# A graph network on one core: the second half of the gates' layer norm stands in the next graph's gates

## The chip, the cores and the metric

The kernel runs on one core of a Trainium2 chip. The metric is device time in microseconds (us) of one execution. The core has five engines that run at the same time, each through its own queue, in the order of that queue: PE (TensorE, matrix products), DVE (VectorE), ACT (ScalarE), POOL (GpSimd) and SP (SyncE, which here only issues transfers). An instruction that waits holds up all that stands behind it in its queue. Transfers (DMA) are issued from the queues of SP, ACT and POOL.

## The reference

The input is 64 graphs of 256 nodes with 256 features, and one 256 x 256 adjacency matrix for each. Two layers follow one another, each with a residual and a layer norm without weights:

```python
def _layernorm(x, axis=-1, eps=1e-5):
    m = jnp.mean(x, axis=axis, keepdims=True)
    v = jnp.var(x, axis=axis, keepdims=True)
    return (x - m) / jnp.sqrt(v + eps)
...
x = _layernorm(x + _L0_gnn_ref(x, adj, ...), axis=-1)
x = _layernorm(x + _L1_gnn_ref(x, adj, ...), axis=-1)
```

Layer 0 is a product with the normalised adjacency matrix and one with a weight matrix. Layer 1 has a convolution branch (a 1 x 1 convolution, then one of 17 taps along the nodes, a residual), a message branch (attention from distances, times messages), and a GRU cell that joins them:

```python
x_in = jnp.concatenate([x_conv, x_nmp], axis=-1)
gi = x_in @ w_ih.T + b_ih
gh = x @ w_hh.T + b_hh
...
r = jax.nn.sigmoid(gi_r + gh_r)
z = jax.nn.sigmoid(gi_z + gh_z)
nn_ = jnp.tanh(gi_n + r * gh_n)
return (1.0 - z) * nn_ + z * x
```

The last line, plus the residual, goes through the second layer norm and is the output. "The gates" below are the GRU cell with that norm.

## The kernel before, in words

The graphs are worked on in four groups (`q`) of 16 (`Q`). A group passes through: layer 0 and the branches of layer 1 for each graph (`layer0`, `layer1`); the products of the long convolution in a transformed domain, for all 16 graphs at once (`products`); the inverse transform, which is DVE work (`complex_end` and what it calls); and the gates graph by graph (`gates`, `gru`). The groups overlap. Each of these is a Python generator that gives control back at every `yield`; a part between two yields is called a piece here. The driver at the end of the kernel interleaves the pieces of one group's gates with the pieces of the next group's `layer0` and `layer1`, with steps of `products`, and (through `paced`) with steps of the inverse transform, which are issued behind instructions that were marked with `mark`. The gates of the last group run after all else, beside the rest of the inverse transform and then alone.

The framework sets the semaphores. It also orders each engine's queue by itself: an instruction that comes earlier in the program takes precedence, but one that is ready may pass one that isn't. `tc.issue_after` forces an instruction behind another one on its engine; `behind`, called in `transposed` for some graphs, does so for all later DVE instructions with respect to a transposition (L812).

`gru(g)` has four pieces. The matrix products (L856) follow a scheme with seven products of 128 x 384 blocks in place of eight, so that some of their operands are sums of blocks that POOL makes beforehand (`input_sums`, L838), and that DVE adds results (L873, L874, L882, L884, L921).

- Piece 1: the load of the next graph's inputs (L787, and L790 for one channel); products p1 and p7; ACT copies p1 (L867).
- Piece 2: product p6, two additions on DVE (L873, L874), the rest of p1, which ACT copies (L876).
- Piece 3: `transposed(g + 1)` (on PE with L824 on ACT, or on DVE at L812 with L813 on POOL and L816 on ACT), the load of this graph's residual into a tile `x1_g` of which there are two (`load_x1`, L794 on SP's queue), product p5 and the rest of p7, additions L882 and L884, three of the next graph's sums on POOL.
- Piece 4: the rest of p5, the fourth sum, a load for the graph after the next one (`load_conv`, L777 or L783), the squashing of the r and z gates on ACT (L897, twice), and `finished`: six elementwise steps on DVE (L905 to L915) with a tanh on ACT (L913), then the layer norm in place on the `x1_g` tile, and the store of the result, issued from ACT's queue (L917).

The layer norm (`layernorm`, L325 to L333) is a generator with one yield. Before it: mean and variance by DVE for two chunks of 128 nodes (L325, L326), an addition (L327), and the power -0.5 on POOL (L328), which gives `ln_rs`. Behind it: the product of the mean with that factor on DVE (L331, `ln_mr`) and the application on ACT, one instruction for each chunk (L333). Its small tiles have four buffers each. In layer 0 the driver takes the two halves at different pieces: statistics at piece 6 of one graph's `layer1`, the rest at piece 2 of the next one. In the gates both halves run in one go (`run`, L916).

For the very last graph the two chunks are finished one after the other.

Of the kernel before, what the change touches and what calls it, by code (L numbers as in the profile page):

```python
# [14 lines left out]
P = 128  # L15
LN_EPS = 1e-5
# [10 lines left out]
def kernel(  # L27
# [27 lines left out]
    nc = tc.nc  # L55
# [35 lines left out]
    def mark(op, gates=0):  # L91
        marks.append((op.ins, gates))
# [7 lines left out]
    def behind(op):  # L100
        order.close()
        order.enter_context(tc.issue_after(op.ins))
# [664 lines left out]
    def in_blocks(g):  # L767
        return g % Q < EARLY or g >= B - Q
# [23 lines left out]
    def load_x1(g):  # L792
        OWN[g] = gate.tile([P, NCH, D], F32, name="x1_g")
        nc.sync.dma_start(OWN[g], x1_d[g // Q][g % Q].rearrange("(c p) d -> p c d", p=P))  # L794
# [12 lines left out]
    def transposed(g):  # L807

        inputs = GATE[g]
        xcT = inputs[:, 2 * DCH :]  # L810
        if in_blocks(g):
            behind(nc.vector.transpose(xcT.rearrange("p k (s r) -> p k s r", r=RB), CONV.pop(g)))  # L812
            nc.gpsimd.tensor_tensor(xcT, xcT, inputs[:, 0 : 2 * DCH : 2 * DCH - 1], op=ALU.add)  # L813
            nc.gpsimd.memset(inputs[0:1, 0], 1.0)
            for k in range(DCH):
                nc.scalar.activation(xcT[:, k], xcT[:, k], AF.Relu, bias=bn2_bias[:, k : k + 1])  # L816
            return
        xc = CONV.pop(g)
        p = bank("p_xcT").rearrange("p (k n) -> p k n", k=DCH)
        for k in range(DCH):  # L820
            for c in range(NCH):
                nc.tensor.transpose(p[:, k, c * P : (c + 1) * P], xc[:, c, k * P : (k + 1) * P], ident)
        for k in range(DCH):
            nc.scalar.activation(xcT[:, k], p[:, k], AF.Relu, bias=bn2_bias[:, k : k + 1])  # L824
# [5 lines left out]
    def input_sums(g, *which):  # L830
        A11, A12, A21, A22 = halves(GATE[g])
        S = SUMS.setdefault(g, {})
        for i in which:
# [3 lines left out]
            }[i]  # L837
            nc.gpsimd.tensor_tensor(S[i], x, y, op=op)  # L838

    def gru(g):  # L840

        following = g % Q + 1 < Q
        inputs, S = GATE.pop(g), SUMS.pop(g)
        G = gate.tile([P, NCH, 2, 4, HD], F32, name="G", bufs=1)
        if following:
            load_gate(g + 1)
        A11, A12, A21, A22 = halves(inputs)

        def product(a, b, p=None):
            first = p is None
            if first:
                p = accbank("p_g")
            for k in range(HALF):
                nc.tensor.matmul(  # L856
                    p[:, : 3 * HD] if k == 0 else p[:, HD:], a[:, k], wall[:, b, k].rearrange("p t d -> p (t d)"),
                    start=first and k == 0, stop=True, skip_group_check=not first or k > 0,
                )
            return p  # L860

        def quarter(c, h):
            return G[:, c, h].rearrange("p t d -> p (t d)")

        p1 = product(A11, B11)
        first = gate.tile([P, 4 * HD], F32, name="first", bufs=1)
        nc.scalar.copy(first, p1)  # L867
        p7 = product(S[3], T3)
        yield
        if following:  # L870
            sent(g + 1)
        p6 = product(S[2], T2)
        mark(nc.vector.tensor_add(quarter(0, 1), first, p6), 1)  # L873
        nc.vector.tensor_add(quarter(1, 1), quarter(0, 1), p7)  # L874
        product(A12, B21, p1)
        nc.scalar.copy(quarter(0, 0), p1)  # L876
        yield
        if following:
            transposed(g + 1)
        load_x1(g)  # L880
        p5 = product(S[1], T1)
        mark(nc.vector.tensor_add(quarter(1, 1), quarter(1, 1), p5), 1)  # L882
        product(A22, T4, p7)
        mark(nc.vector.tensor_add(quarter(1, 0), quarter(0, 1), p7), 1)  # L884
        if following:
            input_sums(g + 1, 3, 1, 2)
        yield
        product(S[4], B22, p5)
        if following:
            input_sums(g + 1, 4)  # L890
        if g % Q + 2 < Q:
            load_conv(g + 2)
        x1 = OWN.pop(g)

        def squashed(c):
            rz = G[:, c, :, GR : GZ + 1, :].rearrange("p h t d -> p h (t d)")
            nc.scalar.activation(rz, rz, AF.Tanh, scale=0.5)  # L897

        squashed(1)

        def finished(part):
            both = G[:, part].rearrange("p c h t d -> p (c h) t d")
            chunks = both.shape[1] // 2
            r, z, n, i = (both[:, :, j, :] for j in (GR, GZ, GN, GI))
            nc.vector.scalar_tensor_tensor(n, r, 1.0, n, op0=ALU.add, op1=ALU.mult)  # L905
            i4 = i.rearrange("p (c h) d -> p c h d", h=2)
            bias = bn_t.rearrange("p (h d) -> p h d", h=2).unsqueeze(1).to_broadcast([P, chunks, 2, HD])
            nc.vector.tensor_tensor(i4, i4, bias, op=ALU.add)
            nc.vector.scalar_tensor_tensor(i, n, 0.5, i, op0=ALU.mult, op1=ALU.add)
            y = x1[:, part]  # L910
            yq = y.rearrange("p c (h d) -> p (c h) d", h=2)
            mark(nc.vector.scalar_tensor_tensor(yq, z, 3.0, yq, op0=ALU.add, op1=ALU.mult), 1)
            nc.scalar.activation(i, i, AF.Tanh)  # L913
            nc.vector.scalar_tensor_tensor(i, z, 1.0, i, op0=ALU.subtract, op1=ALU.mult)
            nc.vector.tensor_sub(yq, yq, i)  # L915
            run(layernorm(y, 4 * LN_EPS))  # L916
            nc.scalar.dma_start(out[g].rearrange("(c p) d -> p c d", p=P)[:, part], y)  # L917

        if g == B - 1:
            finished(slice(1, 2))  # L920
        mark(nc.vector.tensor_add(quarter(0, 1), quarter(0, 1), p5), 1)  # L921
        squashed(0)
        finished(slice(0, 1 if g == B - 1 else NCH))
        yield

# [25 lines left out]
    def run(stage):  # L951
        for _ in stage:
            pass
# [103 lines left out]
    def gates(q, part):  # L1057

        for i in part:
            if i == 0:  # L1060
                load_conv(q * Q)
                load_gate(q * Q)
                yield
                load_conv(q * Q + 1)
                sent(q * Q)
                yield
                transposed(q * Q)
                yield
                input_sums(q * Q, 3, 1, 2, 4)
                yield  # L1070
            yield from gru(q * Q + i)

    def nothing():
        return iter(())
# [15 lines left out]
    for q in range(NQ):  # L1090
        first = (q + 1) * Q
        more = q + 1 < NQ
        end = chain(complex_end(q), copies(V2) if more else iter(()))
        if more:
            if q:
                others = [take(late, 3 if i % 3 == 0 else 2) for i in range(AHEAD)]
            else:
                others = [nothing() for _ in range(AHEAD)]
                ALONE.update(range(first, first + AHEAD))
            TILES[0] = V2  # L1100
            begin = graphs(first, range(AHEAD), others)
        KBANK[0] = bank if q else accbank
        sums(0)
        real = real_transform()
        for step in range(STEPS):
            if step < 4:
                run(products(step))
            else:
                run(merge(products(step), take(real, 1)))
                run(complex_begin(step))  # L1110
            if q:
                run(take(late, (0, 1, 1, 1, 1, 1, 2, 1, 2, 1, 2, 1)[step] if more else step % 2))
            else:
                run(take(begin, 3))
        run(real)
        if not q:
            run(paced(begin, end, RATES[q]))
        elif more:
            run(paced(chain(merge(take(late, 20), take(begin, 6), 3), begin), end, RATES[q]))
        else:  # L1120
            run(paced(late, end, RATES[q]))
            run(end)
        if more:
            run(late)
            run(end)
            if q == 0:
                scope.close()
                gate = ctx.enter_context(tc.tile_pool(name="gate", bufs=2))
            early = gates(q, range(EARLY))
            others = [take(early, 5 if q == 0 else 2) for _ in range(Q)]  # L1130
            run(graphs(first, range(AHEAD, Q), others))
            run(early)
            if q == 0:
                scope, AHEAD, V2 = open_ahead(6)
                ctx.enter_context(scope)
            late = gates(q, range(EARLY, Q))
        else:
            run(gates(q, range(Q)))
    order.close()


# [51 lines left out]
```

## Time and profile before

| what | value |
|---|---|
| median of 3 runs | 2126.97 us (2122.22 to 2134.46) |
| the profiled execution's own time | 2127.71 us |
| its span, first to last instruction | 2125.9 us |
| mean granted PE clock in the span | 0.988 |
| L331 on DVE: instructions, median length | 129, 161 ns |
| L333 on ACT in the gates: instructions, median length | 128, 599 ns |
| L328 on POOL: busy, mean length | 94.9 us, 736 ns |
| L838 on POOL (the sums): busy | 139.9 + 70.2 us |
| stores L917: number, size | 63 of 256 KB, 2 of 128 KB |

Of the instructions in this table, all of L917, half of L333 and 65 of the 129 L331 belong to the gates; the others are layer 0's. A group of instructions is written as line, engine, operation, and output<-inputs by the program's names. In a waits view, "A <- B: 7.7, 4, 3.1" says that A's engine stood idle 7.7 us in total, 4 times, at most 3.1 us, until B released it. In an order of time, a line gives the start, the length, the engine, the line of code, the operation and its tiles, how many were merged into it, and in brackets the idle time of the engine before it with what ended it. A wait for several things is put down to the one that came last.

### The profile page before, as it was taken

Reading aid. Unit: us, or ns where it says so; the run is one execution under the profiler, and the core shown is the slowest. Engines: PE = TensorE matmul, PEld = TensorE weight load, DVE = VectorE, ACT = ScalarE, POOL = GpSimd, SP = SyncE. Lnnn points to the kernel's source line nnn. Section 1 sums busy time; section 2 is a strip of 40 time slices with the busy share of each in tenths; the row PEclk is TensorE's granted clock in tenths of the full one; section 3 lists DMA queues with packets and bytes.
Section 4 is the critical chain, followed back from the end, with each engine's and each line's share of the span. In section 5 each row is a group of like instructions: output and inputs, shape, how many; then the busy total and the mean of one; then the engine's idle time right before and its main releaser. Section 6 shows DMA issues by size and latency. Waiting matters only on the chain. (4 is left out here: it accounts for less than half of the span.)

```text
span 2125.9 us, 26260 instructions
## 1 busy us (share of the span) xinstructions
PE 2006.1 (94%) x8157; PEld 1443.2 (68%) x8157; DVE 1474.1 (69%) x3347; ACT 905.3 (43%) x2114; POOL 666.8 (31%) x672
## 2 busy tenths in 40 slices
PE   6999999888999999999999999999999999899997
PEld 5888788766667756667777666667777765555554
DVE  5555567775558788774556888875445889977776
ACT  4666643456432234555553123446554123233333
POOL 3445310121431243223321234323232123344443
PEclk9999999999999999999999999999999999999999
DMA  4766556433437645344335655334323754443331
GB/s 125 230 210 200 192 183 209 154 132 119 122 96 226 194 123 139 114 120 120 94 99 179 201 155 140 118 104 134 96 93 100 243 146 131 111 118 95 93 94 56
DMA packets 305289, 298.05 MB, mean 140 GB/s; under 512 B 84192, under 2 KB 283956, under 8 KB 305150
## 3 DMA queue, kind: packets, MB, share of 16 engines
q1 hardware_dynamic: 245198, 200.37, 32.1%
q10 hardware_dynamic: 44480, 67.39, 8.9%
q0 software_dynamic: 15472, 28.61, 6.0%
q8 instruction: 66, 1.08, 0.2%
q14 instruction: 73, 0.60, 0.1%
HBM read 193.19 MB, written 103.06 MB: 139 GB/s over the span
## 5 line engine op out<-in xcount | busy, mean ns | idle before, releaser
L856 PE MATMUL p_g<-wall,sums 128*128 128x384 f32 x1536 | 537.7, 489 | 11.6 <-DVE G L882 11.6
L856 PE MATMUL p_g<-wall,inputs 128*128 128x384 f32 x1152 | 409.4, 492 | 14.5 <-DVE G L874 14.1
L856 PEld LDWEIGHTS p_g<-wall,sums 128*128 128x128 f32 x1536 | 284.6, 191 | 200.3 <-issue 19.1
L856 PEld LDWEIGHTS p_g<-wall,inputs 128*128 128x128 f32 x1152 | 218.5, 192 | 167.5 <-DVE G L874 23.4
L838 POOL TENSOR_TENSOR sums<-inputs 128x384 f32<-128x384 f32 x128 | 139.9, 1093 | 343.2 <-PE p_g L856 296.9
L369 POOL TENSOR_TENSOR dis<-deg,neg_half 128x2 f32<-128x2 f32 x64 | 48.3, 754 | 475.7 <-DVE deg L367 468.6
L897 ACT ACTIVATE G<-G 128x512 f32<-128x512 f32 x128 | 80.7, 630 | 250.8 <-DVE G L884 148.6
L328 POOL TENSOR_TENSOR ln_rs<-ln_rs,neg_half 128x2 f32<-128x2 f32 x129 | 94.9, 736 | 275.1 <-DVE ln_rs L327 226.7
L541 PE MATMUL p_k<-u,VM 128*128 128x256 f32 x736 | 175.8, 381 | 4.1 <-DMA u<-ud 4.1
L541 PEld LDWEIGHTS p_k<-u,VM 128*128 128x128 f32 x736 | 139.4, 191 | 31.3 <-DMA u<-ud 3.9
L446 PE MATMUL p_conv<-wc,xn 128*128 128x259 f32 x512 | 130.4, 392 | 22.7 <-DVE xn L430 21.5
L399 PE MATMUL p_hT<-adjT,x 128*128 128x256 f32 x512 | 126.7, 391 | 15.6 <-ACT msg L470 8.2
L333 ACT ACTIVATE x_g<-x_g,ln_mr,ln_rs 128x256 f32<-128x256 f32 x128 | 70.0, 593 | 150.3 <-DVE ln_mr L331 148.3
L446 PEld LDWEIGHTS p_conv<-wc,xn 128*128 128x128 f32 x512 | 94.2, 191 | 53.1 <-DVE xn L430 31.1
L508 DVE TENSOR_TENSOR aT<-aT,adjT 128x512 f32<-128x512 f32 x64 | 44.8, 699 | 123.0 <-ACT aT L507 122.8
L409 PE MATMUL p_out<-w,hT 128*128 128x256 f32 x512 | 123.7, 384 | 3.4 <-ACT hT L404 3.0
L482 PE MATMUL p_dft<-fwd,h 128*128 128x240 f32 x512 | 117.4, 372 | 9.2 <-ACT scols L450 8.8
L515 PE MATMUL p_nmp<-aT,msg 128*128 128x256 f32 x512 | 122.6, 383 | 0.7 <-DVE aT L508 0.7
L467 PE MATMUL p_msg<-wmsg,xn 128*128 128x256 f32 x512 | 122.0, 381 | 0.0
L838 POOL TENSOR_TENSOR sums<-inputs,sums 128x384 f32<-128x384 f32 x64 | 70.2, 1097 | 161.3 <-PE p_g L856 160.6
L331 DVE SCALAR_TENSOR_TENSOR ln_mr<-ln_mv,ln_rs 128x2 f32<-128x2 f32 x129 | 47.3, 368 | 101.7 <-POOL ln_rs L328 101.7
L409 PEld LDWEIGHTS p_out<-w,hT 128*128 128x128 f32 x512 | 95.6, 190 | 29.9 <-ACT hT L404 9.9
(160 smaller groups left out, 3642.0 us busy)
## 6 DMA issues: line engine op xcount, KB each, us to landing
u<-ud SPq DMA_DIRECT2D x284, 256.0 KB
xn_d<-xn ACTq DMA_DIRECT2D x64, 512.0 KB
inputs<-xn_d SPq DMA_DIRECT2D x64, 512.0 KB
ud<-u_set POOLq DMA_DIRECT2D x39, 480.0 KB, 6.3
adj_t<-in_adj_dram SPq DMA_DIRECT2D x64, 256.0 KB
x_t<-in_x_dram SPq DMA_DIRECT2D x64, 256.0 KB
x_d<-x ACTq DMA_DIRECT2D x64, 256.0 KB
xc_d<-VM SPq DMA_DIRECT2D x64, 256.0 KB
```

The source lines that it names most:

```text
L328: nc.gpsimd.tensor_tensor(rs[:, : len(chunks)], rs[:, : len(chunks)], neg_half[:, : len(chunks)], op=ALU.pow)
L333: nc.scalar.activation(y[:, c, :], y[:, c, :], AF.Identity, bias=mr[:, c : c + 1], scale=rs[:, c : c + 1])
L399: nc.tensor.matmul(p[:, k, :], x1[:, mc, k * P : (k + 1) * P], adjT[:, mc, 1 - mc : 3 - mc, :].rearrange("p n q -> p (n q)"), start=mc == ...
L409: nc.tensor.matmul(p[:, c, :], hT[:, k, c * P : (c + 1) * P], w0[:, k, :], start=k == 0, stop=k == DCH - 1)
L446: nc.tensor.matmul(p, x1T[:, k, c * P : (c + 1) * P], wc1[:, k, :], start=k == 0, stop=k == DCH - 1)
L467: nc.tensor.matmul(p[:, c, :], x1T[:, k, c * P : (c + 1) * P], wmsg[:, k, :], start=k == 0, stop=k == DCH - 1)
L482: nc.tensor.matmul(p[:, t0 * FL : t1 * FL], h[:, c, k * P : (k + 1) * P], fwd[:, first : first + t1 - t0, :].rearrange("p t f -> p (t f)") ...
L515: nc.tensor.matmul(p[:, k, :], msg[:, mc, k * P : (k + 1) * P], aT[:, mc].rearrange("p n q -> p (n q)"), start=mc == 0, stop=mc == NCH - 1,)
L541: nc.tensor.matmul(p[:, j * D : (j + 1) * D], v[:, k, :], u[:, k, :], start=k == 0, stop=k == DCH - 1)
L838: nc.gpsimd.tensor_tensor(S[i], x, y, op=op)
L856: nc.tensor.matmul(p[:, : 3 * HD] if k == 0 else p[:, HD:], a[:, k], wall[:, b, k].rearrange("p t d -> p (t d)"), start=first and k == 0, ...
L897: nc.scalar.activation(rz, rz, AF.Tanh, scale=0.5)
```

## The change

The gates' norm is split at its yield. `finished` starts the norm, which runs the statistics and POOL's power, and puts the generator on a list. The remainder (L331, the two L333 and the store) is run by `ended()`, which stands in piece 3 of the next graph's `gru`, behind `transposed(g + 1)` and ahead of `load_x1(g)`. At the last graph `ended()` also stands between the two chunks, and at the end of the kernel. For the last graph of a group the next `gru` is the first one of the next group.

```diff
+    NORMS = []
+
+    def normed(g, part, y):
+
+        yield from layernorm(y, 4 * LN_EPS)
+        nc.scalar.dma_start(out[g].rearrange("(c p) d -> p c d", p=P)[:, part], y)
+
+    def ended():
+        while NORMS:
+            run(NORMS.pop(0))
+
     def gru(g):
...
         if following:
             transposed(g + 1)
+        ended()
         load_x1(g)
         p5 = product(S[1], T1)
...
             nc.vector.tensor_sub(yq, yq, i)
-            run(layernorm(y, 4 * LN_EPS))
-            nc.scalar.dma_start(out[g].rearrange("(c p) d -> p c d", p=P)[:, part], y)
+            NORMS.append(normed(g, part, y))
+            next(NORMS[-1])
 
         if g == B - 1:
             finished(slice(1, 2))
+            ended()
         mark(nc.vector.tensor_add(quarter(0, 1), quarter(0, 1), p5), 1)
         squashed(0)
         finished(slice(0, 1 if g == B - 1 else NCH))
...
             run(gates(q, range(Q)))
+    ended()
     order.close()
```

## The prediction

> **What bounds the kernel now.** I read the page first, then busy time by stage, then the waits of each stage, then the order of time around a norm. The first line gives the engine that sets the end, the three windows give three kinds of stage (columns: length, then busy time of PE, weight loads, DVE, ACT, POOL, granted clock, DMA share, GB/s).
>
> ```profile
> PE 2006.1 (94%) x8157; PEld 1443.2 (68%) x8157; DVE 1474.1 (69%) x3347; ACT 905.3 (43%) x2114; POOL 666.8 (31%) x672
> ...
> 880.00:1150.00 270.00, 259.58 (x1133) 193.71 (x1132) 156.20 (x411) 143.25 (x359) 77.59 (x83) 1.00 0.39 117
> ...
> 1740.00:1880.00 140.00, 125.12 (x394) 71.83 (x393) 130.64 (x261) 42.30 (x79) 50.16 (x49) 0.98 0.44 120
> 1880.00:2126.00 246.00, 232.30 (x718) 135.41 (x716) 174.24 (x326) 87.82 (x157) 107.53 (x118) 0.98 0.35 88
> ```
>
> PE is at 94% of the span, so only its idle 120 us can be won, and half of that (49 and 11 us) lies before the first gates at 560 us or in the drain. Where gates run between layer-1 pieces (880 to 1150, and its twin 1390 to 1650) PE lacks about 10 us of each window. Where they run beside the inverse transform (1740 to 1880) DVE is at 93% and PE lacks 15. In the pure gates after 1950 PE is full up to the drain, and nothing is to be had.
>
> The wait that the change is about, from the views of L331 and of x_g:
>
> ```profile
>   POOL ln_rs L328: 101.7, 116
> ...
>   DVE ln_mr L331: 148.3, 64
> ...
> PE p_g L856 <- DVE G L874: 7.7, 4, 3.1
> PE p_g L856 <- DVE G L882: 6.9, 5, 2.1
> DVE ln_mr L331 <- POOL ln_rs L328: 3.4, 9, 0.8
> ```
>
> DVE stands 101.7 us before the product with the mean, for POOL's power, over all norms of both layers; ACT stands 148.3 us before the gates' 64 applications. These are sums over engines that mostly have slack. The last three lines are the waits of 1740 to 1880: there the DVE wait is 3.4 us in 9 graphs, and PE loses 14.6 us to two DVE additions, of which only L882 (6.9 us) has L331 ahead of it in the queue; L874 stands before L331 (1778.62 against 1779.54 us).
>
> **What an application costs in the mixed stage.** Order of time around two norms (start, length, engine, line, and in brackets the idle time before):
>
> ```profile
> 1025.06 1.22 DVE L331 SCALAR_TENSOR_TENSOR ln_mr<-ln_mv,ln_rs 128x2 f32<-128x2 f32 x1 [0.66 <-POOL ln_rs L328]
> ...
> 1026.31 1.09 ACT L333 ACTIVATE x_g<-x_g,ln_mr,ln_rs 128x256 f32<-128x256 f32 x2 [3.00 <-DVE ln_mr L331]
> ...
> 1027.31 0.36 ACT L449 ACTIVATE h<-p_conv 128x256 f32<-128x256 f32 x1
> ...
> 1028.08 1.89 PE L482 MATMUL p_dft<-fwd,h 128*128 128x240 f32 x8 [0.66 <-ACT scols L450]
> ...
> 1030.94 1.99 PE L399 MATMUL p_hT<-adjT,x 128*128 128x256 f32 x8 [0.75 <-ACT msg L470]
> ...
> 211.37 0.16 DVE L331 SCALAR_TENSOR_TENSOR ln_mr<-ln_mv,ln_rs 128x2 f32<-128x2 f32 x1 [1.70 <-POOL ln_rs L328]
> 211.60 0.38 ACT L449 ACTIVATE h<-p_conv 128x256 f32<-128x256 f32 x1 [0.55 <-PE p_conv L446]
> ...
> 213.13 1.12 ACT L333 ACTIVATE x<-x,ln_mr,ln_rs 128x256 f32<-128x256 f32 x2
> ```
>
> At 1026 ACT stands 3.00 us for L331, then applies a gates norm, and only then copies conv 1 out (L449), although the matmuls for it had begun at 1023.3; PE pays 0.66 and 0.75 us behind it. The last three lines show what the program place does: layer 0's norm is already in two parts, and its application goes behind L449. They show also what it doesn't do: its L331 still waits 1.70 us for POOL. Program place is a precedence, not a slot: an engine's queue takes what is ready (the next graph's L873 stands between two L326 of the norm at 1777.58).
>
> **The change part by part.** No instruction is added or removed: per graph it moves one L331 (0.16 us alone), two L333 (1.09 us) and one store (0.38 us of issue on ACT's queue) behind the next graph's transposition, ahead of L882. Statistics and power stay.
>
> 1. Mixed stages. The PE waits right behind a gates application, all on ACT's copies (L450, L470): 2.19, 0.66, 0.75, 0.82, 0.75 us between 923 and 1110, and 2.19, 1.31, 0.75, 0.67, 0.76 between 1430 and 1581: 10.9 us. Upper end: all go, as at 211 to 213 us. Lower end: 0, if ACT is still free when the application becomes ready, so that it keeps its slot. The rows lie on both sides, so I take half, 5.4 us.
>
> 2. DVE stage, 1740 to 1880. The wait of 3.4 us goes if transform pieces fill it; at 93% DVE a microsecond of DVE is one of the stage: 3.2 us. Ends: 0 (the next DVE instruction waits for PE instead, as L884 does for 2.8 us) and 6.9 (every PE wait on L882).
>
> 3. First pure gates, 1880 to 1950. DVE waits 2.11 us a graph before L331 with L882 behind it, and PE waits 2.1 us in all for L882. Ends 0 and 2.1; I take 1.0. The L882 waits in the earlier gates (1.7 and 0.9 us) are counted for the upper end alone.
>
> 4. Cost. L331 now stands in L882's own piece. PE waits for L882 in 5+1+1+4 = 11 graphs; there L331's 0.16 us is on the path: 1.8 us. The applications pass ACT's squash L897, covered by ACT's idle 2.58 us before it at 1784.20; without that cover 1.09 us a graph. The store passes SP's queue: the next but one load_x1 (L794) needs its buffer. It is issued at 2073.71, 2.4 us after the store of 2071.32, and behind it stand L790 and the convolution loads, then POOL's L813 and the sums L838, which PE needs from 2089 on and which are done by 2085.7: 3.4 us of cover, so I cost it at nothing. Behind POOL's power nothing changes.
>
> [...]
>
> ```profile
> 1779.48 0.99 POOL L838 TENSOR_TENSOR sums<-inputs 128x384 f32<-128x384 f32 x1
> 1779.54 0.95 DVE L331 SCALAR_TENSOR_TENSOR ln_mr<-ln_mv,ln_rs 128x2 f32<-128x2 f32 x1 [0.23 <-POOL ln_rs L328]
> ```
>
> L331 lasts 0.95 us there, not 0.16, since POOL's next sum begins with it; six of the stage's nine L331 are so, 6 x 0.79 = 4.7 us of DVE. I count none of it as won, because the transform step L623 at 1795.79, beside such a sum, lasts 1.23 us and not its usual 0.41: whatever takes L331's place is held as long. [...]
>
> Sum: 5.4 + 3.2 + 1.0 - 1.8 = 7.8 us from the profiled execution's 2127.71 (span 2125.9): 2119.9. The runs' median, 2126.97, lies 0.7 lower, so 2119. Lower ends throughout, with the cost, give 2129; all upper ends (10.9 + 6.9 + 2.1 + 2.6) give 2105.
>
> **The rivals.**
> - No change. L331 takes the place that it has, because DVE is idle when POOL's power ends; layer 0's rows speak for it (split, and 1.70 us still waited), the row of its application behind L449 against. Time: 2126 to 2127.
> - All of it: every application yields to L449 and L470, and L331 leaves L882's path: 2105. For it speaks the row at 213.13; against it that L331 still precedes L882 in the program.
> - Slower, through the store. If precedence drops the application behind both squashes (L897 at 2072.64 and 2074.57, 0.63 us each), the store leaves at 2075.20 + 1.09 = 2076.3 instead of 2071.3: 5.0 us later. L794 waits so much longer at the head of SP's queue, the one-channel load and the convolution loads behind it, then L813 and the sums. Beyond the cover of 3.4 us it decides: 1.6 us in each of the last 17 graphs, 27 us, less the 7 us won earlier: 2148. For it: L794 already waits (up to 3.39 us on a semaphore), and PE's weight loads already wait 10.8 us for L838. Against: ACT is idle 1.3 us and more before each squash, so the application is likely to fit in.
>
> **How the numbers follow.** What a measurement of this kernel can tell from no change is about 0.5%, 10.6 us (its three runs span 12). Forecast 45%, its own range 2112 to 2126, a third of it below 2116. No change 18%. All of it 13%. Slower through the store 24%, a twelfth of that still within 10.6 us. So faster 0.15 + 0.13 = 0.28, same 0.30 + 0.18 + 0.02 = 0.50, slower 0.22. The range 2105 to 2146 leaves out half of "all of it" and half of the slower case, 0.19. The forecast lies within what counts as the same.
>
> **What would show it.** Part 1: the PE waits on L470 and L450 between 880 and 1150 fall from 5.2 us to about half, and L449 stands ahead of the gates' L333. Part 2: in 1740 to 1880 the 3.4 us vanish and PE's wait on L882 shrinks by about as much, L331 lying behind transform steps. Part 4: L794 and the POOL sums keep their distance to PE, and weight loads wait no more than now for L838. The prediction is wrong if the L331 wait stays at 101.7 us with the same order (no change), or if POOL waits longer for its loads after 1880 (slower).

## The result: no change, and the profile after

| kernel | median us (range, runs) | profiled execution, span | mean granted PE clock |
|---|---|---|---|
| before, beside it | 2131.56 (2118.93 to 2138.72, 20) | 2125.9 | 0.988 |
| changed | 2130.30 (2122.49 to 2137.67, 20) | 2127.6 | 0.987 |

The ratio is 0.9998, 95% interval 0.9986 to 1.001. The change is worth less than 3 us either way. 2119 and a gain of 7.8 us were forecast, counted from the 2126.97 that the three earlier runs of the kernel before had. In the changed kernel the lines behind the diff stand lower down: L856 is now L867, L874 is L885, L882 is L894, L884 is L896, L897 is L909. Lines up to L836 are the same.

The page's line of engine totals (busy us, share of the span, instructions), and the windows that the prediction used (columns as there):

```profile
PE 2008.2 (94%) x8157; PEld 1447.5 (68%) x8157; DVE 1466.9 (69%) x3347; ACT 904.1 (42%) x2114; POOL 668.2 (31%) x672
```

```profile
880.00:1150.00 270.00, 255.95 (x1097) 189.97 (x1096) 148.20 (x392) 140.52 (x355) 75.32 (x81) 0.98 0.36 106
...
1740.00:1880.00 140.00, 128.91 (x418) 74.62 (x417) 139.10 (x272) 42.84 (x80) 58.97 (x52) 1.00 0.46 124
1880.00:2128.00 248.00, 236.12 (x733) 138.78 (x731) 174.29 (x333) 90.60 (x162) 110.34 (x119) 0.98 0.36 90
```

The totals say that nothing happened: PE's idle time is 119.4 us, it was 119.8. The windows say that much did. Between 880 and 1150 PE gets through 1097 matmuls where it did 1133, and its clock is 0.98, not 1.00. Between 1740 and 1880 it gets through 418 where it did 394, at 1.00 and not 0.98. A sum over the span hides two effects of opposite sign.

Windows at fixed times compare different work. So the stages are cut at the same instructions in every kernel: at the first and the last product of the long convolution of each group (L541), and at the last store of the inverse transform's result for the group. "Inverse" is gates beside the inverse transform, "mixed" is gates beside `layer0` and `layer1` of the next group. Two stages, before and then after, with the length in the second column:

```profile
942.37:1138.11 195.74, 189.68 (x834) 141.74 (x833) 99.63 (x263) 108.44 (x275) 61.74 (x66) 1.00 0.36 105
...
1722.06:1873.28 151.22, 136.34 (x431) 78.92 (x430) 142.17 (x273) 43.36 (x80) 55.39 (x52) 0.98 0.42 113
```

```profile
941.92:1148.13 206.21, 194.42 (x835) 144.90 (x834) 97.72 (x263) 108.31 (x275) 61.25 (x66) 0.98 0.35 99
...
1734.06:1878.16 144.10, 133.00 (x431) 77.46 (x431) 141.10 (x273) 43.19 (x80) 58.97 (x52) 1.00 0.45 119
```

The matmul counts (834 and 835, 431 and 431) show that the same work is compared. All stages from the first product on, as length / idle time of PE, in us (k is the products of a group, with its number; the groups count from 0):

| stage | before | after | difference of length |
|---|---|---|---|
| k0 and mixed 0 (from 283 us on) | 353.05 / 30.21 | 353.67 / 30.75 | +0.6 |
| k1 | 108.23 / 2.32 | 110.46 / 2.99 | +2.2 |
| inverse 1 | 198.38 / 7.75 | 194.93 / 5.32 | -3.4 |
| **mixed 1** | 195.74 / 6.06 | 206.21 / 11.79 | **+10.5** |
| k2 | 113.21 / 4.18 | 112.78 / 4.79 | -0.4 |
| inverse 2 | 199.83 / 7.56 | 196.64 / 5.32 | -3.2 |
| **mixed 2** | 189.70 / 6.88 | 195.79 / 9.87 | **+6.1** |
| k3 | 81.21 / 3.36 | 80.72 / 2.81 | -0.5 |
| inverse 3 | 151.22 / 14.88 | 144.10 / 11.10 | -7.1 |
| gates alone, end | 252.6 / 13.6 | 249.4 / 11.5 | -3.2 |

The three inverse stages win 13.7 us, the two mixed ones give back 16.6. Three programs were later profiled twice; their two profiles agree within 1.0 us in mixed 1, mixed 2 and inverse 3 and within 1.6 us in inverse 1, but differ by up to 2.1 us in inverse 2, 2.4 in k3 and 3.4 in the gates alone. So the last row, and the k rows, are not told from chance by one profile; the bold rows are.

### The profile page after: what moved, and what is told of

Read it like the earlier page. It is cut to its first block, busy times and chain, and to the rows that moved or that the text cites. A ratio compares the mean times of both kernels' runs of the same rounds, so it can differ in the third digit from the quotient of the medians.

```text
span 2127.6 us, 26255 instructions
## 1 busy us (share of the span) xinstructions
PE 2008.2 (94%) x8157; PEld 1447.5 (68%) x8157; DVE 1466.9 (69%) x3347; ACT 904.1 (42%) x2114; POOL 668.2 (31%) x672
## 5 line engine op out<-in xcount | busy, mean ns | idle before, releaser
L867 PE MATMUL p_g<-wall,sums 128*128 128x384 f32 x1536 | 535.9, 488 | 5.0 <-DVE G L894 4.8
L867 PE MATMUL p_g<-wall,inputs 128*128 128x384 f32 x1152 | 407.0, 489 | 14.2 <-DVE G L885 14.2
L867 PEld LDWEIGHTS p_g<-wall,sums 128*128 128x128 f32 x1536 | 284.1, 190 | 192.1 <-issue 13.3
L867 PEld LDWEIGHTS p_g<-wall,inputs 128*128 128x128 f32 x1152 | 217.9, 191 | 164.9 <-DVE G L885 21.2
L909 ACT ACTIVATE G<-G 128x512 f32<-128x512 f32 x128 | 80.8, 631 | 251.1 <-DVE G L896 151.9
L541 PE MATMUL p_k<-u,VM 128*128 128x256 f32 x736 | 175.7, 381 | 3.6 <-DMA u<-ud 3.5
L541 PEld LDWEIGHTS p_k<-u,VM 128*128 128x128 f32 x736 | 139.5, 191 | 30.9 <-DMA u<-ud 4.8
L399 PE MATMUL p_hT<-adjT,x 128*128 128x256 f32 x512 | 129.3, 396 | 9.8 <-DVE adjT L381 8.1
L482 PE MATMUL p_dft<-fwd,h 128*128 128x240 f32 x512 | 120.3, 379 | 18.1 <-ACT scols L450 18.1
L409 PE MATMUL p_out<-w,hT 128*128 128x256 f32 x512 | 128.1, 395 | 5.3 <-ACT hT L404 4.8
L409 PEld LDWEIGHTS p_out<-w,hT 128*128 128x128 f32 x512 | 98.2, 195 | 33.4 <-ACT hT L404 13.1
L482 PEld LDWEIGHTS p_dft<-fwd,h 128*128 128x128 f32 x512 | 98.1, 195 | 32.5 <-ACT scols L450 24.0
L333 ACT ACTIVATE x_g<-x_g,ln_mr,ln_rs 128x256 f32<-128x256 f32 x128 | 70.9, 597 | 111.6 <-DVE ln_mr L331 110.2
```

What stands on the lines that cost most here:

```text
L333: nc.scalar.activation(y[:, c, :], y[:, c, :], AF.Identity, bias=mr[:, c : c + 1], scale=rs[:, c : c + 1])
L399: nc.tensor.matmul(p[:, k, :], x1[:, mc, k * P : (k + 1) * P], adjT[:, mc, 1 - mc : 3 - mc, :].rearrange("p n q -> p (n q)"), start=mc == ...
L409: nc.tensor.matmul(p[:, c, :], hT[:, k, c * P : (c + 1) * P], w0[:, k, :], start=k == 0, stop=k == DCH - 1)
L482: nc.tensor.matmul(p[:, t0 * FL : t1 * FL], h[:, c, k * P : (k + 1) * P], fwd[:, first : first + t1 - t0, :].rearrange("p t f -> p (t f)") ...
L541: nc.tensor.matmul(p[:, j * D : (j + 1) * D], v[:, k, :], u[:, k, :], start=k == 0, stop=k == DCH - 1)
L867: nc.tensor.matmul(p[:, : 3 * HD] if k == 0 else p[:, HD:], a[:, k], wall[:, b, k].rearrange("p t d -> p (t d)"), start=first and k == 0, ...
```

## What happens in a mixed stage

The waits of PE in mixed 1, before and then after (total us, times, longest):

```profile
PE p_hT L399 <- ACT msg L470: 2.3, 3, 0.8
...
PE p_dft L482 <- ACT scols L450: 0.7, 1, 0.7
```

```profile
PE p_dft L482 <- ACT scols L450: 6.6, 3, 2.6
...
PE p_hT L399 <- ACT msg L470: 0.3, 1, 0.3
```

One wait behind the gates' application went as it was meant to (L399, 2.3 to 0.3), another grew ninefold (L482, 0.7 to 6.6). The same places in mixed 2: 1.5 to 0.3, and 2.0 to 4.5. Two waits at the first gates of each of these stages are new as well, 1.4 us for DVE's L499 and 0.9 us for ACT's L404 (at 964 and 966 us in mixed 1); e1 below, with the norm whole there, has neither. The order of time around the norm that the prediction showed at 1025 us, in the changed kernel:

```profile
1028.21 0.70 POOL L328 TENSOR_TENSOR ln_rs<-ln_rs,neg_half 128x2 f32<-128x2 f32 x1 [5.53 <-DVE ln_mv L326]
1028.87 1.27 POOL L392 TENSOR_TENSOR x_t<-x_t,b_t 128x512 f32<-128x512 f32 x1
1030.10 0.71 POOL L328 TENSOR_TENSOR ln_rs<-ln_rs,neg_half 128x2 f32<-128x2 f32 x1
...
1030.84 1.02 DVE L331 SCALAR_TENSOR_TENSOR ln_mr<-ln_mv,ln_rs 128x2 f32<-128x2 f32 x2 [2.36 <-POOL ln_rs L328]
1031.82 1.09 ACT L333 ACTIVATE x<-x,ln_mr,ln_rs 128x256 f32<-128x256 f32 x2 [4.63 <-DVE ln_mr L331]
1032.82 0.36 ACT L449 ACTIVATE h<-p_conv 128x256 f32<-128x256 f32 x1
...
1033.29 2.50 PE L482 MATMUL p_dft<-fwd,h 128*128 128x240 f32 x8 [2.65 <-ACT scols L450]
...
1034.16 1.11 ACT L333 ACTIVATE x_g<-x_g,ln_mr,ln_rs 128x256 f32<-128x256 f32 x2
```

The gates' application (x_g) did yield: it stands behind the conv 1 copies now, at 1034.16. But the slot ahead of the copies is not empty. Layer 0's application (x) has it. Before, the gates' L331 waited 0.66 us for its power; layer 0's application came after the copies. Now both L331 run together, behind the second power, which is layer 0's, and that one stands on POOL behind layer 0's bias addition (L392, 1.27 us). ACT waits 4.63 us where it waited 3.00, with the copies queued behind, and PE 2.65 where it waited 0.66. The same order recurs at 1075.7 and 1115.6.

The waits can cost more than their length. The granted clock in windows of 5 us behind the second of these waits (2.64 us, ended at 1076.16):

```profile
1070.00:1075.00 5.00, 3.52 (x19) 2.73 (x17) 2.33 (x11) 0.37 (x2) 3.56 (x4) 1.00 0.54 186
1075.00:1080.00 5.00, 3.84 (x13) 3.34 (x14) 1.03 (x5) 4.49 (x13) 0.00 (x0) 0.66 0.32 108
1080.00:1085.00 5.00, 5.00 (x21) 3.04 (x20) 1.94 (x5) 2.54 (x8) 0.00 (x0) 1.00 0.16 52
```

A window at 0.66 is 5 x 0.34 = 1.7 us of PE lost; such a stretch is called a dip here. Mixed 1 has three dips (965 to 970 at 0.66, 1030 to 1040 at 0.96 and 0.70, 1075 to 1080 at 0.66) and mixed 2 two (at 0.50 from 1481.76 to 1485.17, and 1550 to 1555 at 0.66); before, neither had one (1.00 over both stages). That adds up to the stages: mixed 1 is 5.7 us of idle time plus 3 x 1.7 = 10.8 (measured 10.5), mixed 2 is 3.0 plus 3.4 = 6.4 (measured 6.1). In inverse 3 it runs the other way: before had two dips (1745 to 1755 at 0.83 and 0.82, 1810 to 1820 at 0.82 and 0.84), the change has none (1.00 over the stage), 3.8 + 3.5 = 7.3 (measured 7.1). Those 3.5 us belong to this profile rather than to the kernel. In e2, e4 and r4 below the norm is whole in this stage, PE's waits on the two additions are the same 7.7 and 6.9 us, there is no dip, and the stage takes 147.9 us. So what the split wins there for certain is the 3.8 us of waiting; whether a dip is saved as well depends on how a wait falls (last section). The dips of mixed 1 are not fixed either: between 1000 and 1150 us e2, split there too, has one (1035 to 1040, at 0.66), the change two.

## The experiments

All leave the computation whole. Where a line of a conv 1 copy is L451, the edit has moved it by one from L450. The theories at the start: **A**, order: the gain belongs to the inverse stages, the loss to layer 0's norm, which takes the gates' slot in the mixed stages. **B**: the differences between stages are chance, mostly of the clock. **C**: the gates' own application, at its new place, is what stands in the way. The first four ran beside one set of runs of before (2130.38 us).

### e1, e2: split only outside, or only inside, the mixed stages

`EARLY` is 4: the gates of the first four graphs of a group run in the mixed stage. e1 runs the norm in one go where the graph or the next one is of these, and splits it elsewhere; e2 does the opposite.

```diff
+        def mixed(g):
+            return g % Q < EARLY and g < B - Q
...
             NORMS.append(normed(g, part, y))
             next(NORMS[-1])
+            if mixed(g) or mixed(g + 1):          # e2: if not (...)
+                ended()
```

> Theory A (order): the split wins 10 to 16 us where the gates run beside the inverse transform and alone, and loses as much where they run between layer-1 pieces, because layer 0's application then stands ahead of conv 1's copies (L449) and is ready later. With the norm whole for the gates graphs 0 to 3 of a group (and the one before them) and split elsewhere: 10 to 16 us below before, ratio 0.992 to 0.996. Theory B (chance: the stage differences between the two profiles are clock losses that fall anywhere): ratio 0.998 to 1.002.

> The converse: split only for the gates graphs that run between layer-1 pieces. Theory A: 9 to 16 us above before, ratio 1.004 to 1.008, with PE's wait on L450 between the third products and the second gates grown from 2.7 to about 11 us over both mixed stages. Theory B: 0.998 to 1.002.

Measured: e1 2121.16 us, ratio 0.996 (0.9945 to 0.9975); e2 2144.68 us, ratio 1.0081 (1.0061 to 1.0102). By stages (length / PE idle):

| stage | before | after | e1 | e2 |
|---|---|---|---|---|
| inverse 1 | 198.4 / 7.8 | 194.9 / 5.3 | 194.9 / 5.3 | 197.9 / 7.0 |
| mixed 1 | 195.7 / 6.1 | 206.2 / 11.8 | 198.2 / 8.2 | 205.4 / 12.4 |
| inverse 2 | 199.8 / 7.6 | 196.6 / 5.3 | 195.2 / 5.3 | 200.2 / 7.6 |
| mixed 2 | 189.7 / 6.9 | 195.8 / 9.9 | 190.6 / 7.9 | 197.3 / 11.3 |
| inverse 3 | 151.2 / 14.9 | 144.1 / 11.1 | 144.2 / 11.2 | 147.9 / 14.8 |

B falls: the two halves of the change have opposite signs, each beyond its interval, and the mixed stages are long where their norm is split. The two don't add up, though: e1's gain is 8.5 us and e2's loss 17.3, and the change, which has both, differs from before by less than 3. The profile of e2 is that of its fastest run, 9 us below its median, so its stages don't show where that loss lies, and it stays open. Nor does e1's mixed 1 come back to 195.7 us, with the norm whole there: it takes 198.2, for a reason that the runs don't show.

### e3, e4: layer 0's remainder held behind the conv 1 copies

e3 is the changed kernel, e4 the kernel before, both with layer 0's applications (L333) forced behind the newest copy of conv 1 (L450). The order is forced on ACT alone, the engine of that copy: L331, on DVE, is not held.

```diff
-            nc.scalar.copy(cols[:, c, :, :NSE], ...)
+            COPIED[0] = nc.scalar.copy(cols[:, c, :, :NSE], ...).ins
...
                 if piece == APPLIED:
-                    run(ENDS.pop())
+                    with tc.issue_after(COPIED[0]):
+                        run(ENDS.pop())
```

> The change as it is, and layer 0's remainder forced behind conv 1's copies (L450) on ACT. Theory A: the new wait on L450 goes, 8 to 16 us below the changed kernel, ratio 0.992 to 0.997 to before. Theory C (the loss in the mixed stage comes from the gates' own application standing ahead of L470): no gain, 0.998 to 1.003.

> Control: the kernel before with the same order forced. There layer 0's application already stands behind L450 in the graphs in which a gates norm ends, so theory A expects little: ratio 0.998 to 1.003. If it gains as much as the run with the split, the gain there has nothing to do with the split.

Measured: e3 2128.81 us, 0.9997 (0.9985 to 1.001), nothing won; e4 2127.46 us, 0.9987 (0.9974 to 1.0). A, as put, misses: layer 0's application is out of the way in e3, and mixed 1 still takes 204.3 us. The time is the one that C named, though not its place: PE waits 0.6 us for L470 there, and 5.1 for the copies. The same place in e3's order of time:

```profile
1029.81 1.02 DVE L331 SCALAR_TENSOR_TENSOR ln_mr<-ln_mv,ln_rs 128x2 f32<-128x2 f32 x2 [2.36 <-POOL ln_rs L328]
...
1030.91 0.60 ACT L333 ACTIVATE x_g<-x_g,ln_mr,ln_rs 128x256 f32<-128x256 f32 x1 [4.75 <-POOL sums L839]
1031.42 0.36 ACT L450 ACTIVATE h<-p_conv 128x256 f32<-128x256 f32 x1
...
1031.89 2.60 PE L483 MATMUL p_dft<-fwd,h 128*128 128x240 f32 x6 [2.02 <-ACT scols L451]
```

With layer 0's application gone the gates' application is back in the slot, and since its L331 still comes late (2.36 us), the copies wait as long (4.75 us). So the theory was put anew, **A'**: whichever application stands ahead of the conv 1 copies holds them until its own L331 is through, and both L331 wait for the later power. Its rival, **D**: it is DVE's stall itself that costs, wherever the applications stand.

### e5, e6, e7, e8: the parts apart

These ran on another chip, beside runs of before at 2131.49 us. e5 puts e1 and e3's hold together. e6 splits all norms and holds the applications of both norms behind the copies in the mixed stages. e7 leaves all where the change has it and moves layer 0's bias addition (L392) behind the newest power on POOL. e8 leaves L331 where it was before, and moves only the two applications and the store to the next graph's third piece.

```diff
# e6, besides e3's edit
-        ended()
+        if g % Q < EARLY and g < B - Q:
+            with tc.issue_after(COPIED[0]):
+                ended()
+        else:
+            ended()
         load_x1(g)
# e7 (POWER[0] is the newest L328)
-        nc.gpsimd.tensor_tensor(x_t, x_t, b0_t..., op=ALU.add)
+        with tc.issue_after(POWER[0]) if g > Q + 2 else ExitStack():
+            nc.gpsimd.tensor_tensor(x_t, x_t, b0_t..., op=ALU.add)
# e8, in the gates' norm
         nc.gpsimd.tensor_tensor(rs..., op=ALU.pow)
-        yield
         mr = small.tile([P, NCH], F32, name="ln_mr")
         nc.vector.scalar_tensor_tensor(mr..., op0=ALU.mult, op1=ALU.mult)
+        yield
```

> The norm whole where gates run between layer-1 pieces, split elsewhere, and layer 0's remainder behind conv 1's copies. If the two gains (8.5 us and 2.9 us) are separate: 9 to 12 us below before, ratio 0.994 to 0.996. If they are the same inverse-transform time twice: 0.996 to 0.997.

> Split everywhere, with layer 0's and, in the mixed stages, the gates' remainder both forced behind conv 1's copies (L450) on ACT. Theory A', corrected: whichever application stands ahead of L450 holds it until the L331 behind it in DVE's order is through. Then with none ahead of L450 the mixed stages come back to 196 and 190 us or below (206 and 196 in the change): ratio to before 0.990 to 0.995. Theory D (the loss is DVE's 2.4 us stall before L331 itself, not ACT's order): the mixed stages stay above 202 and 194, ratio 0.998 to 1.001.

> The change, with layer 0's bias addition on POOL (1.27 us) forced behind the last power, so that it no longer stands between the gates' power and layer 0's. Theory A': the wait before L331 falls from 2.4 to about 1.1 us in the three affected graphs of each mixed stage, and with it the wait on L450: 4 to 8 us below the change, 0.996 to 0.998. If POOL's order doesn't matter: 0.999 to 1.001.

> The split moved by one instruction: the product with the mean (L331) stays with the statistics, only the two applications and the store stand in the next graph's third piece. Theory A': the loss in the mixed stages comes from L331 falling behind layer 0's; here the gates' L331 keeps its place and its short wait (0.7 us), so the mixed stages are as before or shorter (190 to 196 and 184 to 190 us): 0.993 to 0.998. Theory C (it is the moved application): the mixed stages as in the change, 206 and 196, ratio 0.998 to 1.002.

| kernel | median us | ratio (interval) | inverse 1 | mixed 1 | mixed 2 | inverse 3 |
|---|---|---|---|---|---|---|
| e5 | 2112.36 | 0.9918 (0.9904 to 0.9933) | 194.7 | 198.8 | 190.4 | 144.0 |
| e6 | 2117.50 | 0.9943 (0.9923 to 0.9962) | 194.7 | 198.9 | 192.6 | 144.2 |
| e7 | 2125.81 | 0.9976 (0.9961 to 0.999) | 199.5 | 201.0 | 194.6 | 144.0 |
| e8 | 2142.53 | 1.0058 (1.004 to 1.0076) | 198.2 | 207.6 | 197.6 | 152.3 |

**e6** tells A' and D apart. Its order of time at the same place:

```profile
1025.05 0.38 ACT L450 ACTIVATE h<-p_conv 128x256 f32<-128x256 f32 x1 [0.71 <-PE p_conv L447]
...
1027.89 1.78 PE L483 MATMUL p_dft<-fwd,h 128*128 128x240 f32 x8
1027.98 1.02 DVE L331 SCALAR_TENSOR_TENSOR ln_mr<-ln_mv,ln_rs 128x2 f32<-128x2 f32 x2 [2.35 <-POOL ln_rs L328]
1028.97 0.60 ACT L333 ACTIVATE x<-x,ln_mr,ln_rs 128x256 f32<-128x256 f32 x1 [2.59 <-DVE ln_mr L331]
```

DVE stands 2.35 us as in the change (13.1 us in all of mixed 1, 13.2 in the change). But the copies run 2.9 us before L331, L483 waits for nothing, and the stage is 7.3 us shorter. D falls; it is the place on ACT ahead of the copies that costs. Mixed 1 doesn't come back to the expected 196 us: PE's wait for L470 (L471 here) is back, 2.6 us with an application ahead of it, and waits of 1.7 us for L405, 1.4 for L500 and 1.1 for L380 stand where before had none.

**e7** shortens the wait at its root. With line numbers moved (L485 is L482, L453 is L450), PE's wait for the copies in mixed 1, and DVE's for the power, are

```profile
PE p_dft L485 <- ACT scols L453: 2.4, 3, 1.4
...
DVE ln_mr L333 <- POOL ln_rs L330: 9.4, 10, 1.1
```

instead of 6.6 with up to 2.6; the second line is the wait of L331 (L333 here), 13.2 with up to 2.4 in the change. No order on ACT was touched, so the lateness of the power behind L392 is part of the cause, as A' has it. Mixed 1 is 5.2 us shorter than in the change; mixed 2 gains only 1.2, and inverse 1 is 4.6 us longer, at a granted clock of 0.97 against 1.00, with PE busy for 193.7 us against 189.6.

**e8** misses A', which expected it to spare the mixed stages; they are as long as in the change or longer, and its ratio lies above the ranges of both theories. The order shows why (L452 and L453 are the copies, L449 and L450 before):

```profile
1079.71 0.60 ACT L336 ACTIVATE x_g<-x_g,ln_mr,ln_rs 128x256 f32<-128x256 f32 x1 [3.00 <-DVE ln_mr L332]
...
1081.56 0.60 ACT L336 ACTIVATE x<-x,ln_mr,ln_rs 128x256 f32<-128x256 f32 x1 [1.25 <-DVE ln_mr L332]
1082.06 0.36 ACT L452 ACTIVATE h<-p_conv 128x256 f32<-128x256 f32 x1
...
1082.54 0.67 PE L485 MATMUL p_dft<-fwd,h 128*128 128x240 f32 x2 [2.37 <-ACT scols L453]
```

L332 (the old L331) comes as early as before, yet one application of each norm now stands ahead of the first copy (L452), each behind its own wait. So here theory C has a share: a moved application does harm also with an early product. What stays of A' is its first half: an application ahead of the copies holds them for as long as it waits itself, for whichever power. What e8 settles is inverse 3. PE's waits there on the two additions are 7.7 and 6.9 us, as before, and its idle time 14.7 (before 14.9, the change 11.1): moving applications and store on ACT wins nothing there, and the gain needs L331's move on DVE. In inverse 1 it is not all of it: PE is idle for 6.8 us in e8, 7.8 before and 5.3 in the change, and its wait for L882 is 0.4 us in e8 as in the change, where it was 1.7. That L331 alone, without the applications, would win as much was not run.

### Once more on one chip, and both cures together

On the first two chips e1 and e4 multiply to 0.996 x 0.9987 = 0.9947; e5 had 0.9918, below the range that was expected of it. So e1, e4 and e5 were run again side by side (as r1, r4, r5; before 2130.05 us), with e9, which is e6 and e7's edit together.

> The same program as e1 (whole norm where gates run between layer-1 pieces, split elsewhere), beside e5 and e4 on one chip. If the two savings simply add, this ratio times that of r4 is that of r5: 0.996 x 0.999 = 0.995. If layer 0's application in front of conv 1's copies costs more when the other stages are faster, r5 stays at 0.992 and the product at 0.995. Expected here 0.996, within 0.002.

> The same program as e4 (the kernel before, layer 0's remainder behind conv 1's copies). Theory A' (an application ahead of conv 1's copies costs only where its product with the mean comes late) gives little here, since in the kernel before layer 0's application mostly stands behind the copies already: 0.997 to 1.000.

> The same program as e5. If the two savings add: 0.995, some 2120 us. If they do more together: 0.992, some 2113 us. A mean apart from the product of r1 and r4 by more than 0.002 on this chip too says that they do.

> Norm split at all graphs, both remainders behind conv 1's copies in the mixed stages (e6), and layer 0's bias addition on POOL behind the newest power (e7's edit). Theory A' : e6 still had L331 wait 13.1 us in the first mixed stage, which made the gates' remainder late but not conv 1's copies; with the bias out of the way the waits fall and the remainders fit in, 0.991 to 0.994 against before, below or at e6's 0.9943. Rival (DVE's stall or the bias addition's lateness takes its place: layer 0's next weight product waits for it): above e6, 0.995 to 0.999.

| kernel | median us | ratio (interval) |
|---|---|---|
| r1 | 2121.62 | 0.9959 (0.9942 to 0.9975) |
| r4 | 2131.26 | 0.9999 (0.9983 to 1.0015) |
| r5 | 2113.89 | 0.9924 (0.9902 to 0.9946) |
| e9 | 2114.83 | 0.9937 (0.9915 to 0.9959) |

All three repeat within their intervals. The product of r1 and r4 is 0.9958, r5 is 0.0034 below it: more than the 0.002 put down beforehand, though about the size of the three intervals taken together. The stage table doesn't say where it lies: mixed 1 and mixed 2 of e1 and e5 agree within 1 us in both pairs of profiles (r1 and r5 are the second), and the rest is spread over stages that differ as much between two profiles of one program. That the hold is worth more on e1 than on the kernel before is likely, and its cause stays open.

e9 is not told from e6 (0.9937 and 0.9943). In it the wait of layer 0's application for L331 in mixed 1 fell as expected, from 10.1 to 6.4 us, but the rival was seen too, in PE's waits of mixed 1 (L413 is L409, layer 0's weight product):

```profile
PE p_out L413 <- ACT hT L408: 2.4, 2, 1.9
```

PE's idle time there is 7.0 us against e6's 9.1, and a clock of 0.98 against 1.00 takes it back: 198.7 against 198.9 us. e5 has the lowest ratio in both rounds, 0.8% below before, though e9's interval overlaps with its own: split where DVE is the bound, whole where ACT's order matters, and layer 0's remainder behind the copies.

## Why the prediction was wrong

**Part 1, the mixed stages (forecast -5.4, ends 0 and -10.9): this is the step that failed.** Both ends asked only whether the gates' application keeps its slot or leaves it. In the mixed stages it left, and the waits on L470 that the prediction listed went: 2.3 to 0.3 and 1.5 to 0.3. The two of 2.19 us at 923 and 1430 us lie in the inverse stages. There the application kept its slot ahead of L470, and PE waits 1.2 us at that place for DVE's L381 instead. What was not asked is who stands next in the program. Layer 0's remainder was quoted in its place behind L449, as evidence that a split norm goes there. But that place wasn't fixed either: with the gates' remainder gone from in front, it moved ahead of the copies and brought its own later power along, and L482's waits rose from 2.7 to 11.1 us over both stages. With the clock's dips the two stages lost 16.6 us. "Program place is a precedence, not a slot" was in the prediction; the conclusion, that a lower precedence for one instruction is a higher one for another, was not drawn. The lower end of 0 excluded a loss without a reason.

**Part 2, the inverse stages beside DVE (forecast -3.2, ends 0 and -6.9): right in mechanism; that the stage won more is in part luck.** L331 no longer waits in the window from 1740 to 1880, a transform step (L623) fills its place, and PE's waits on the two additions are

```profile
PE p_g L867 <- DVE G L885: 7.1, 6, 1.6
PE p_g L867 <- DVE G L894: 4.0, 3, 1.7
```

11.1 us, where they were 14.6. The 3.5 us is what was forecast. The stage won 7.1, since two dips of the clock (3.5 us), which in this profile of before stood behind waits of 3.07 and 2.47 us on L874, went as well; three other profiles (e2, e4, r4) have the same waits without a dip, so the prediction lacked a term for the clock, but its size here is partly luck. A gain exists in the two earlier inverse stages too (3.4 and 3.2 us, of which 2.4 and 2.2 are idle time of PE), which the prediction split up between part 1's list and a remark on L882. By e8 the gain in inverse 3 needs L331's move; in inverse 1 the fall of the wait on L882, from 1.7 to 0.4, doesn't.

**Part 3 (forecast -1.0):** PE's waits on that addition after 1873 us, 2.1 before, are no longer in the list. The stage is 3.2 us shorter, and two profiles of one program differ by as much (3.4). The prediction's "2.11 us a graph" before L331 was the longest of five waits that add up to 9.3.

**Part 4 (forecast +1.8, and nothing for the store):** the cost of L331 ahead of L894 isn't seen; over the whole span PE waits 4.8 us for L894, where it waited 11.6 for L882. The slower rival, the store in front of SP's loads, didn't come: in the last stage POOL's inputs waited 54.0 us for their loads, before 60.5, and over the span PE's weight loads waited 6.7 us for the sums, before 10.8. The row of the long L331 was borne out: at 1789.51 it again lasts 0.96 us beside a sum (1.01 us from 1789.43), and six of the nine L331 from 1740 to 1882 last 0.95 to 0.98 us, six of nine as before. At 1866.53, where it lasts 0.15 us, the transform step behind it (L728, 0.42 us in the median) lasts 1.18 us beside the sum that runs from 1866.51 to 1867.54.

Against the kernel before, the time is what the rival "no change" gave, but not for its reason: L331 did leave its place (its wait for POOL fell from 101.7 to 92.6 us, in 89 places and not 116). The views that the prediction watched were L331 and the gates' application; what grew is in the third line here, layer 0's application, which waited 17.7 us in 12 places before:

```profile
ACT x_g L333 <- DVE ln_mr L331: 110.2, 50, 5.1
DVE ln_mr L331 <- POOL ln_rs L328: 92.6, 89, 2.4
ACT x L333 <- DVE ln_mr L331: 53.9, 21, 4.6
```

The first two sums fell, from 148.3 and 101.7, as hoped for; the third tripled, 33.0 us of it in the two mixed stages, in front of conv 1's copies. Nothing in the mechanism makes gain and loss equal; that they cancel to within 3 us is chance.

## What to carry to other kernels

Where an order is by precedence, putting one instruction later promotes whatever stands behind it: before pricing a move, name the next candidate for the slot, and what that one waits for. A change that is the same in every stage should be priced by stage, and if the signs differ, be made only where it pays: here 0.9998 became 0.996 by a condition on the graph's number, and 0.992 with the promoted neighbour held back as well. When totals don't move, cut the spans at the same instructions and compare lengths before believing that nothing happened.

## What the runs showed of the hardware

PE waits of 3.07 and 2.47 us (before, until 1747.25 and 1813.65) and of 2.65, 2.64 and 2.55 us (after, until 1033.29, 1076.16 and 1548.54) each had some 3.4 us at half clock beside them, which began between 0.6 us ahead of the wait's end and 1.5 us behind it, seen as windows of 5 us at 0.66, or two that add up to it; those of 2.14 us (before, at 1848.71) and 1.27 us (after, at 1117.03) had not. The length of a wait doesn't decide it, though. In the kernel before PE waits 2.19 us for L470 twice, until 923.47 and until 1430.61, and only the second wait is followed by a dip. In r4 a wait of 3.07 us, until 1755.43, has none: the clock is 1.00 over its whole inverse 3.

In the profiles of before and after each dip, up to the drain, lasts 3.41 us or twice that (in before 1748.35 to 1751.76 and 519.55 to 526.38, both at 0.50), and in one profile dips begin whole multiples of 3.413 us apart (before, 1748.35 and 1813.20 us: 19 times). So the trace can be cut at this step. The windows around the two waits, cut so (length, busy time of PE, and behind the engines the clock):

```profile
918.91:922.32 3.41, 1.94 (x10) 1.29 (x8) 2.77 (x13) 0.68 (x2) 0.92 (x1) 1.00 0.10 36
922.32:925.74 3.42, 2.27 (x10) 1.94 (x11) 1.76 (x7) 3.31 (x9) 0.00 (x0) 1.00 0.36 122
...
1427.50:1430.91 3.41, 0.79 (x4) 0.50 (x4) 2.81 (x14) 1.90 (x4) 0.91 (x1) 1.00 0.00 0
1430.91:1434.32 3.41, 3.41 (x9) 2.70 (x8) 0.74 (x2) 2.02 (x6) 0.00 (x0) 0.50 0.69 233
```

The wait at 923 is divided between two windows, in which PE is idle for 1.5 and 1.2 us. The one at 1430 lies in one window, which with another short wait is idle for 2.6, and the next window runs at half clock. In the profiles of before and after, cut so from 30 to 2110 us, all sixteen windows at full clock in which PE was idle for over 2.0 us (2.02 to 3.41) had one at half clock behind them, and none with less than 1.7 us had; of the eight from 1.70 to 1.97 us three had. That also covers the dips at 965 and 1480 us in the change, which have no long wait behind them: of three waits there (0.7, 1.4 and 0.9 us) the last two fall into one window, 2.3 us in all.

So a dip cost 1.7 us beyond the wait (3.41 us at 0.50), and whether a wait of some 2 to 3 us brought one went with where it fell; in these two profiles none that was below 1.7 us and stood alone in its window did.
